# A four-layer graph network on one core: rows by block transposes and partition broadcasts, one statistics instruction per norm, and a plan with ranks

## The chip, the cores and the metric

The kernel runs on one core of one Trainium2 chip. The metric is the device time of one launch in microseconds. A core has a matrix engine (PE), a vector engine (DVE), a scalar engine (ACT), a general engine (POOL) and a queue that issues the DMAs here (SP); each works through its own instructions in program order and waits on semaphores for the others. PE's weight loads (PEld) stand beside its matmuls. PE writes to PSUM; the other tiles lie in SBUF.

## The reference

There are 64 independent graphs, each with 256 nodes and 256 features, all in fp32. A graph goes through four layers, and each layer ends in a residual sum and a layer norm. Cut to what matters:

```
for each of 64 graphs (x: 256x256, adj: 256x256):
  # layer 0: 4 heads, sigmoid attention scaled by row and column degrees
  q, k, v = lrelu(x Wq), lrelu(x Wk), lrelu(x Wlin + b)
  A_h = adj * sigmoid(q_h k_h^T / 8);  dis_h = rowsum(A_h)^-0.5
  x = norm(x + norm(dis_h * (A_h (dis_h * v_h))))
  # layer 1: 8 heads, masked softmax attention
  x = norm(x + (softmax(mask(q_h k_h^T / sqrt(32))) v_h) Wo + bo)
  # layer 2: neighbour sum, 256 -> 1024, rms norm, silu, 1024 -> 256
  h = (eps x + adj x) W1 + b1
  x = norm(x + silu(h * rsqrt(mean(h^2) + 1e-6) * w) W2 + b2)
  # layer 3: additive attention: e[i,j] = lrelu(s1[i] + s2[j])
  V = x W;  s1, s2 = V a1, V a2
  x = norm(x + gelu(norm(softmax(mask(e)) V) * gamma + beta))
```

Three of these quantities are needed as a row, that is, one value for each node along the free axis and the same on all partitions: the factor rsqrt(...) of layer 2 (hidden features lie on the partitions there), s2 of layer 3, and 1/sum of each head of layer 1 (its output lies with features on the partitions). Each comes into being as a column, with nodes on the partitions.

## The kernel before

**Graphs and operations.** The function `graph` describes one graph as a list of operations, each with an engine, a cost in ns that its author wrote beside it, the values that it reads and writes, and a closure that issues its instructions. `Plan.order` takes the operations of all 64 graphs together and makes one order of them: of those whose inputs are ready it takes the one with the lowest key, and it moves a clock for each engine by the written cost. The order so made is what the engines run. Several graphs are thus under way at once, each in another layer, and PE's work of one covers the other engines' work of the others. The key of an operation is this line, `start` being the earliest start by the plan's clocks and `due` a due time taken from the operations that follow it:

```
key = start, op.due, op.graph, op.index
```

**PE's modes.** Matmuls of layers 0 and 1 use part of the array: rows (L502, L582: queries times keys), or columns (L542, L618: attention times values; L520, L680: sums over partitions). The others use the full array (L368, L379, L649, L661, L707, L722). Transposes (`pe.transpose`, L323, L625, L693, L731) are matmuls against an identity. The plan has a price for each change of mode (`CHANGE`), and after rows or columns it starts operations of another mode later (`STAY`), to keep equal ones together.

**The rows.** In layer 2, `rs` (a column, two blocks of 128 nodes) is spread over 128 columns by a broadcast view and transposed by PE into the PSUM tile `pr` (L693, two instructions); DVE multiplies the hidden features by it (L697). In layer 3 the column s2 is spread in the same way (L731, two instructions, PSUM tile `ps2`), and ACT adds s1 to it and applies the leaky relu (L735). In layer 1, the reciprocals of 16 sums per node (8 heads, two blocks of nodes) are transposed by PE (L625), copied by ACT into `rT` (L627), written to DRAM by one DMA (L628) and read back by eight, one for each head, which spread a row of 256 over 32 partitions (L631, tile `rb`); DVE multiplies `av` by it (L635), which feeds the product with Wo (L379).

**The norms.** `stats` is called six times for each graph. For each of the two blocks of 128 nodes DVE runs `bn_stats` over 256 features (L393) and `bn_aggr` (L395); POOL adds 1e-5 (L405) and raises to the power -1/2 (L406). Where the sums of the softmax of layer 3 are folded in, DVE multiplies the variance twice by 1/sum (L401) and the result once (L409). Then `normed` or `affine` apply mean and factor, on ACT (L420, L445) or on DVE (L424, L453, L456).

**Transposes through DRAM.** Most large transposes aren't PE's: DVE transposes blocks of 32x32 (L335, L603), one DMA writes to a DRAM tile `far`, and four read it back.

**DMAs.** All come from SP's queue, in the plan's order.

Of the kernel before, what the change touches and what calls it, by code (L numbers as in the profile page):

```python
# [29 lines left out]
WORDS = {"s": 516, "d": 1024, "b": 2048, "c": 32, "p": 512, "h": 1024}  # L30
AHEAD = 12
STAY = 200
# [8 lines left out]
SLOTS = {"s": 42, "d": 10, "b": 3, "c": 72, "p": 8, "h": 8}  # L41
# [41 lines left out]
class Plan:  # L83
# [4 lines left out]
    def __init__(self, graphs):  # L88
        self.graphs = graphs
        self.ops, self.turns = [], {}  # L90
        self.graph = 0

    def op(self, engine, cost, fn, w=(), r=(), turn=None, mode="full", after=None, size=0, joint=None):

        pair = lambda x: (x[0], None if x[0].kind == "p" else x[1]) if isinstance(x, tuple) else (x, None)
        w, r = [pair(x) for x in w], [pair(x) for x in r]
        op = Op(engine, cost, fn, w, r, self.graph, turn, mode, after, size)
        op.table, op.joint, op.leaves = turn is not None and engine == "ACT", joint, mode
        if op.table:
            self.turns[turn] = self.turns.get(turn, 0) + 1  # L100
        self.ops.append(op)

# [42 lines left out]
    def order(self):  # L145
# [3 lines left out]
        for op in reversed(self.ops):  # L149
            op.due = min((nxt.due for nxt in op.after), default=4 * (min(op.graph + ROUND[3], self.graphs - 1 + TAIL[3]) + 1))  # L150
            if op.turn is not None:
                op.due = min(op.due, op.turn)
        clock = {e: 0.0 for e in AFTER}
# [6 lines left out]
        while ready:  # L160
            best = None
            for op in ready:
                if (op.due - AHEAD if op.first else op.turn or 0) > turns[turn]:
                    continue
                start = clock[op.engine]
                if op.engine == "PE" and mode in ("rows", "columns") and mode != op.mode:
                    start += STAY - 60 * (op.mode == "transpose")
                start = max(start, op.ready)
                need = {}
                for v in op.values:  # L170
                    if v.slot is None:
                        need[v.kind] = need.get(v.kind, 0) + 1
                for kind, n in need.items():
                    free = self.free[kind]
                    if len(free) < n:
                        break
                    start = max(start, sorted(free)[n - 1][0])
                else:
                    key = start, op.due, op.graph, op.index
                    if best is None or key < best[0]:  # L180
                        best = key, start, op
# [45 lines left out]
def weights(plan, nc, c, t):  # L227
# [32 lines left out]
    column("b1_q", "L1_gnn_bq"), column("b1_v", "L1_gnn_bv"), row("b1_o", "L1_gnn_bo")  # L260
# [37 lines left out]
def graph(plan, nc, c, t, out, b):  # L298
# [57 lines left out]

    def copy(ps, name):
        dst = Value("s", name, 2)
        op("ACT", 466, lambda: act.copy(dst.t, ps.t), [dst], [ps])  # L359
        return dst  # L360
# [26 lines left out]
    def stats(src, r=None):  # L387


        mv, st = Value("c", "mv", 2), Value("c", "st", 2)  # L390
        m = lambda: mv.t[:, :6].rearrange("p (n k) -> p n k", n=2)
        for n in range(NB):
            op("DVE", 328, lambda n=n: dve.bn_stats(st.t[:, 6 * n:6 * n + 6], two(src)[:, n, :]), [(st, n)], [(src, n)])  # L393
        for n in range(NB):
            op("DVE", 82, lambda n=n: dve.bn_aggr(m()[:, n, 0:2], st.t[:, 6 * n:6 * n + 6]), [(mv, n)], [(st, n)])  # L395

        r2 = lambda: r.t[:, :NB]
        if r:
            def fn():
                for _ in range(2):  # L400
                    dve.tensor_tensor(m()[:, :, 1], m()[:, :, 1], r2(), OP.mult)  # L401
            op("DVE", 250, fn, [mv], [mv, r])

        def fn():
            pool.tensor_scalar(m()[:, :, 2], m()[:, :, 1], 1e-5, None, op0=OP.add)  # L405
            pool.tensor_tensor(m()[:, :, 2], m()[:, :, 2], c.mhalf[:, :NB], OP.pow)  # L406
        op("POOL", 1010, fn, [mv], [mv], after=580)
        if r:
            op("DVE", 60, lambda: dve.tensor_tensor(m()[:, :, 2], m()[:, :, 2], r2(), OP.mult), [mv], [mv, r])  # L409
        return mv, m  # L410

    def normed(src, name):
        mv, m = stats(src)
        dst = Value("s", name, 2)
        if name != 'o' or b >= plan.graphs - ENDS:
            op("DVE", 70, lambda: dve.scalar_tensor_tensor(  # L416
                m()[:, :, 0], m()[:, :, 0], -1.0, m()[:, :, 2], op0=OP.mult, op1=OP.mult), [mv], [mv])
        for n in range(NB):
            if name != 'o' or b >= plan.graphs - ENDS:
                op("ACT", 492, lambda n=n: act.activation(  # L420
                    two(dst)[:, n, :], two(src)[:, n, :], AF.Identity, bias=m()[:, n, 0:1], scale=m()[:, n, 2:3]),
                    [(dst, n)], [(src, n), mv])
                continue
            op("DVE", 328, lambda n=n: dve.tensor_scalar(  # L424
                two(dst)[:, n, :], two(src)[:, n, :], m()[:, n, 0:1], m()[:, n, 2:3],
                op0=OP.subtract, op1=OP.mult), [(dst, n)], [(src, n), mv])
        return dst
# [11 lines left out]
    def affine(y, mv, m, g, add, r=(), src=None):  # L439

        if src and b >= plan.graphs - ENDS:
            op("DVE", 70, lambda: dve.scalar_tensor_tensor(
                m()[:, :, 0], m()[:, :, 0], -1.0, m()[:, :, 2], op0=OP.mult, op1=OP.mult), [mv], [mv])
            for n in range(NB):
                op("ACT", 491, lambda n=n: act.activation(  # L445
                    two(y)[:, n, :], two(src)[:, n, :], AF.Identity, bias=m()[:, n, 0:1], scale=m()[:, n, 2:3]),
# [5 lines left out]
        for n in range(NB):  # L452
            op("DVE", 395, lambda n=n: dve.scalar_tensor_tensor(  # L453
                two(y)[:, n, :], two(src)[:, n, :], m()[:, n, 0:1], g.t, op0=OP.subtract, op1=OP.mult),
                [(y, n)], [(src, n), mv, g])
            op("DVE", 395, lambda n=n: dve.scalar_tensor_tensor(  # L456
                two(y)[:, n, :], two(y)[:, n, :], m()[:, n, 2:3], add(n), op0=OP.mult, op1=OP.add),
# [107 lines left out]
    ps = feature_major(c.w1_q, xT)  # L565
    qT1 = Value("s", "qT1", 2)
    for o in range(2):
        op("ACT", 357, lambda ps=ps, o=o: act.activation(
            two(qT1)[:, o, :], two(ps)[:, o, :], AF.Identity, bias=c.b1_q.t[:, o:o + 1]), [(qT1, o)], [(ps, o), c.b1_q])

    kT1 = copy(feature_major(c.w1_k, xT), "kT1")
# [3 lines left out]
    for hq in range(H1 // 4):  # L575
# [9 lines left out]
        for pair in range(2):  # L585
            e = Value("d", "e", 4)
            for i in range(2):
                softmax(pss[2 * pair + i], negmask, HD1 ** -0.5, e,
                        lambda n, i=i, e=e: e.t[:, 256 * (2 * i + n):256 * (2 * i + n + 1)],
                        lambda n, i=i: 2 * i + n, r, lambda n, h=4 * hq + 2 * pair + i: 2 * h + n, turn(1, EXP))  # L590
# [22 lines left out]
    def fn():  # L613
# [10 lines left out]
    ps = Value("p", "ps")  # L624
    op("PE", PE_TR, lambda ps=ps: pe.transpose(ps.t[:16, :P], r.t[:, :16], c.ident), [ps], [r], mode="transpose")  # L625
    rT, far, rb = Value("s", "rT"), Value("h", "far"), Value("s", "rb", H1)
    op("ACT", 160, lambda ps=ps: act.copy(rT.t[:16, :P], ps.t[:16, :P]), [rT], [ps])  # L627
    op("SP", 470, lambda far=far: nc.sync.dma_start(far.t[:2].rearrange("q (g m) -> (q g) m", m=P), rT.t[:16, :P]),  # L628
       [far], [rT], after=2000, size=8)
    for h in range(H1):  # L630
        op("SP", 470, lambda h=h, far=far: nc.sync.dma_start(  # L631
            two(rb)[h % 4 * HD1:(h % 4 + 1) * HD1, h // 4, :],
            far.t[h // 4:h // 4 + 1, h % 4 * N:(h % 4 + 1) * N].to_broadcast([HD1, N])), [(rb, h)], [far], after=1700, size=32)
    yT = Value("s", "yT")
    op("DVE", 575, lambda: dve.tensor_tensor(yT.t, av.t, rb.t, OP.mult), [yT], [av, rb])  # L635
# [3 lines left out]
    for n in range(NB):  # L639
        d = lambda n=n: two(adj2)[:, n, n * P:(n + 1) * P]  # L640
        op("DVE", 200, lambda d=d: dve.tensor_tensor(d(), d(), c.eps_id.t, OP.add), [(adj2, n)], [(adj2, n), c.eps_id])
# [47 lines left out]
    pr = Value("p", "pr")  # L689

    def fn():
        for n in range(NB):
            pe.transpose(pr.t[:, n * P:(n + 1) * P], rs.t[:, n:n + 1].to_broadcast([P, P]), c.ident)  # L693
    op("PE", 2 * PE_TR, fn, [pr], [rs], mode="transpose")
    for j in range(0, HB, 4):
        four = [(hT, i) for i in range(j, j + 4)]
        op("DVE", 1130, lambda j=j: dve.tensor_tensor(  # L697
            Hb(j, 4), Hb(j, 4), pr.t[:, None, :N].to_broadcast([P, 4, N]), OP.mult), four, [*four, pr])
# [28 lines left out]
    ps2 = Value("p", "ps2")  # L727

    def fn():
        for n in range(NB):  # L730
            pe.transpose(ps2.t[:, n * P:(n + 1) * P], V3()[:, n, D + 1:D + 2].to_broadcast([P, P]), c.ident)  # L731
    op("PE", 2 * PE_TR, fn, [ps2], [v3], turn=turn(3, EXP), mode="transpose")
    e = Value("s", "e3", 2)
    for n in range(NB):
        op("ACT", 360, lambda n=n: act.activation(two(e)[:, n, :], ps2.t[:, :N], AF.Prelu, bias=s1(n), alpha=0.2),  # L735
           [(e, n)], [ps2, v3])
# [16 lines left out]
def gnn_stack_kernel(ctx: ExitStack, tc: tile.TileContext, t: dict, out: bass.AP):  # L753
# [20 lines left out]
        {"space": {"p": bass.MemoryType.PSUM, "h": bass.MemoryType.DRAM}[kind]} if kind in "ph" else {})))  # L774
# [4 lines left out]
    make_identity(nc, ident)  # L779
# [57 lines left out]
```

## Time and profile before

| what | value |
|---|---|
| median of 3 runs (2696.18 to 2699.69) | 2696.62 us |
| the profiled execution, first to last instruction | 2698.6 us |
| PE busy, share of the span | 2666.0 us, 99% |
| DVE busy | 2436.7 us, 90% |
| ACT busy | 2228.8 us, 83% |
| POOL busy | 588.5 us, 22% |
| DMA queue of SP, share of 16 engines | 67.0% |
| mean granted TensorE clock | 0.997 |

The page gives no time of its own for the profiled execution beyond its span, which is 2.0 us above the median of the runs. "Busy" counts the time in which at least one instruction of the engine is under way. Matmuls overlap, so a busy PE is read further down by the distance between the starts of its instructions.

### The profile page before, as it was taken

Reading aid. Unit: us, or ns where it says so; the run is one execution under the profiler, and the core shown is the slowest. Engines: PE = TensorE matmul, PEld = TensorE weight load, DVE = VectorE, ACT = ScalarE, POOL = GpSimd, SP = SyncE. Lnnn points to the kernel's source line nnn. Section 1 sums busy time; section 2 is a strip of 40 time slices with the busy share of each in tenths; the row PEclk is TensorE's granted clock in tenths of the full one; section 3 lists DMA queues with packets and bytes.
Section 4 is the critical chain, followed back from the end, with each engine's and each line's share of the span. In section 5 each row is a group of like instructions: output and inputs, shape, how many; then the busy total and the mean of one; then the engine's idle time right before and its main releaser. Section 6 shows DMA issues by size and latency. Waiting matters only on the chain.

```text
span 2698.6 us, 56499 instructions
## 1 busy us (share of the span) xinstructions
PE 2666.0 (99%) x17568; PEld 2144.9 (79%) x17568; DVE 2436.7 (90%) x7480; ACT 2228.8 (83%) x5343; POOL 588.5 (22%) x902
## 2 busy tenths in 40 slices
PE   8999999999999999999999999999999999999997
PEld 6777788887887878878888878888788788787776
DVE  6789999999899999999999999989999899999986
ACT  4888888888888988888888888888888888888886
POOL 1111222212222212222222222222222222222212
PEclk9999999999999999999999999999999999999999
DMA  4476875766767767667767677677676676776661
GB/s 146 133 213 176 219 219 161 211 192 183 200 185 187 215 178 189 196 181 207 202 169 206 186 190 212 173 190 201 172 213 193 169 212 189 186 212 181 169 173 36
DMA packets 708045, 501.01 MB, mean 186 GB/s; under 512 B 309792, under 2 KB 667552, under 8 KB 707744
## 3 DMA queue, kind: packets, MB, share of 16 engines
q1 hardware_dynamic: 707744, 497.40, 67.0%
q8 instruction: 140, 2.29, 0.4%
q14 instruction: 161, 1.32, 0.2%
HBM read 301.35 MB, written 195.82 MB: 184 GB/s over the span
## 4 chain that ended last, share of the span: by engine, by line
PE 93%; DVE 3%; ACT 2%; DMA 1%; SPq 1%; issue 1%; POOL 0%; ACTq 0%; POOLq 0%; DVEq 0%
PE ps L368 16%; PE ps L707 16%; PE ps L661 16%; PE ps L379 15%; PE ps L582 5%; PE ps L502 4%; PE ps L542 4%; PE av L618 4%; PE ps L722 4%; PE ps L649 4%; PE ps L323 1%; PE ps L520 1%; PE pr L693 1%; DVE e L465 1%; PE ps L731 0%
## 5 line engine op out<-in xcount | busy, mean ns | idle before, releaser
L470 ACT ACTIVATE e<-e,low 128x256 f32<-128x256 f32 x1152 | 574.6, 500 | 83.7 <-DVE low L465 82.9
L707 PE MATMUL ps<-w,hT 128*128 128x256 f32 x2048 | 466.8, 380 | 1.3 <-ACT hT L699 1.2
L661 PE MATMUL ps<-aggT,w 128*128 128x256 f32 x2048 | 463.4, 380 | 1.6 <-ACT aggT L359 1.0
L707 PEld LDWEIGHTS ps<-w,hT 128*128 128x128 f32 x2048 | 385.7, 190 | 60.4 <-issue 4.6
L661 PEld LDWEIGHTS ps<-aggT,w 128*128 128x128 f32 x2048 | 383.3, 190 | 57.0 <-issue 2.8
L405 POOL TENSOR_SCALAR mv<-mv 128x2 f32<-128x2 f32 x384 | 127.8, 333 | 1316.8 <-DVE mv L395 888.0
L465 DVE CUSTOM_DVE_ANT_0 e<-ps,adj 128x256 f32<-128x256 f32 x1024 | 361.7, 418 | 30.0 <-PE ps L582 29.9
L406 POOL TENSOR_TENSOR mv<-mv,mhalf 128x2 f32<-128x2 f32 x384 | 306.0, 797 | 32.0
L603 DVE STREAM_TRANSPOSE eb<-e 128x1024 f32<-128x1024 f32 x248 | 300.8, 1221 | 0.8 <-ACT e L470 0.7
L668 ACT ACTIVATE hT<-ps,br,r 128x256 f32<-128x256 f32 x512 | 255.7, 585 | 33.9 <-PE ps L707 30.6
L393 DVE BATCH_NORM_STATS2 st<-y 128x6 f32<-128x256 f32 x640 | 238.3, 408 | 1.2
L420 ACT ACTIVATE x<-y,mv 128x256 f32<-128x256 f32 x384 | 215.2, 600 | 28.9 <-DVE mv L416 26.1
L666 ACT ACTIVATE sq<-ps,b 128x256 f32<-128x256 f32 x512 | 220.0, 474 | 20.2 <-PE ps L661 19.7
L470 ACT ACTIVATION_READ_ACCUMULATOR e<-e,low 128x1 f32 x1152 | 219.0, 190 | 0.0
L508 DVE TENSOR_TENSOR att<-att,adjT 128x512 f32<-128x512 f32 x256 | 166.4, 676 | 10.0 <-ACT att L506 10.0
L688 POOL TENSOR_TENSOR rs<-rs,mhalf 128x2 f32<-128x2 f32 x64 | 45.6, 712 | 540.4 <-DVE rs L686 518.9
L528 POOL TENSOR_TENSOR dp<-dp,mhalf 128x8 f32<-128x8 f32 x64 | 110.2, 1722 | 215.8 <-DVE dp L527 168.3
L697 DVE TENSOR_TENSOR hT<-hT,pr 128x1024 f32<-128x1024 f32 x128 | 150.0, 1210 | 5.2 <-PE pr L693 4.3
L582 PE MATMUL ps<-kT,qT 32*128 32x256 f32 x2048 | 146.2, 399 | 0.0
L673 DVE TENSOR_TENSOR sq<-sq 128x512 f32<-128x512 f32 x192 | 129.5, 675 | 11.1 <-ACT sq L666 10.2
L368 PE MATMUL ps<-x0T,w_q 128*128 128x256 f32 x512 | 130.4, 385 | 6.6 <-DMA x0T<-in_xT 6.6
L506 ACT ACTIVATE att<-ps 128x512 f32<-128x512 f32 x256 | 132.2, 603 | 3.8 <-PE ps L502 3.1
(119 smaller groups left out, 5508.9 us busy)
## 6 DMA issues: line engine op xcount, KB each, us to landing
far<-eb SPq DMA_DIRECT2D x248, 512.0 KB, 3.6
eT<-far SPq DMA_DIRECT2D x992, 128.0 KB, 4.1
adj<-in_adj SPq DMA_DIRECT2D x128, 256.0 KB, 5.1
far<-eb SPq DMA_DIRECT2D x488, 64.0 KB, 2.0
x0T<-in_xT SPq DMA_DIRECT2D x64, 256.0 KB, 4.7
adjT<-in_adjT SPq DMA_DIRECT2D x64, 256.0 KB, 4.9
x<-in_x SPq DMA_DIRECT2D x64, 256.0 KB, 5.2
adj<-in_adjT SPq DMA_DIRECT2D x64, 256.0 KB, 4.8
```

Of the source, the lines that this page charges most:

```text
L368: pe.matmul(two(ps)[:, o, :], w.t[:, k, o * P:(o + 1) * P], two(xT)[:, k, :], start=(k == 0), stop=(k == DB - 1))
L379: pe.matmul(two(ps)[:, n, :], two(xT)[:, k, n * P:(n + 1) * P], w()[:, k, :], start=(k == 0), stop=(k == DB - 1))
L393: op("DVE", 328, lambda n=n: dve.bn_stats(st.t[:, 6 * n:6 * n + 6], two(src)[:, n, :]), [(st, n)], [(src, n)])
L406: pool.tensor_tensor(m()[:, :, 2], m()[:, :, 2], c.mhalf[:, :NB], OP.pow)
L465: op("DVE", 345, lambda n=n: dve.tensor_tensor_reduce(out=E(n), in0=two(logits)[:, n, :], in1=two(negmask)[:, n, :], scale=-scale, scalar= ...
L470: op("ACT", 491, lambda n=n: act.activation(E(n), E(n), AF.Exp, bias=low.t[:, n:n + 1], scale=-1.0, accum_out=r.t[:, col(n):col(n) + 1]), ...
L582: pe.matmul(two(pss[i])[:, n, :], two(qT1)[s, hq, n * P:(n + 1) * P], two(kT1)[s, hq, :], start=True, stop=True)
L603: op("DVE", 1155, lambda e=e, eb=eb: dve.transpose(eb.t.rearrange("p (b g i) -> p g b i", b=4, i=32), e.t.rearrange("p (g b i) -> p g b i" ...
L661: pe.matmul(two(ps)[:, i, :], c.w2_1.t[:, k, (j + i) * P:(j + i + 1) * P], two(aggT)[:, k, :], start=(k == 0), stop=(k == DB - 1))
L666: op("ACT", 357, lambda ps=ps, sq=sq, i=i, j=j: act.activation(two(sq)[:, i, :], two(ps)[:, i, :], AF.Square, bias=c.b2_1.t[:, j + i:j + i ...
L668: op("ACT", 491, lambda ps=ps, i=i, j=j: act.activation(Hb(j + i)[:, 0], two(ps)[:, i, :], AF.Identity, bias=c.br2.t[:, j + i:j + i + 1], ...
L707: pe.matmul(two(ps)[:, n, :], Hb(j)[:, 0, n * P:(n + 1) * P], c.w2_2.t[:, j, :], start=(j == 0), stop=(j == HB - 1))
```

## The change

The rows of layers 2 and 3 are made by a new function, `row_of`: DVE transposes blocks of 32x32 of a broadcast view of the column, after which the first partition of each group of 32 holds 32 values of each block; four POOL instructions (`partition_broadcast`) then copy one group's partition to all 128. The row is a tile in SBUF instead of PSUM. POOL loads a library of instructions for it at the start of the kernel. The identity is made by a POOL `iota` and a DVE comparison, in place of a POOL memset and a POOL selection.

The reciprocals of layer 1 are transposed by DVE in blocks of 32x32 and written to DRAM by one DMA with 128 runs of 64 values; the eight DMAs that spread them read runs of 64 values instead of runs of 256. `yT` is made by two DVE instructions, one for each block of nodes.

`stats` runs one `bn_stats` over both blocks, with the two blocks' features interleaved by the view; its even and odd halves are the two blocks. `bn_aggr` goes. What follows reads the sum of squared deviations (third word of three) and multiplies by 1/256 and adds 1e-5 in one DVE instruction, so POOL keeps only the power. 

Of the smaller edits: the keys of layer 1 get their bias (b1_k), by two ACT instructions instead of one copy; eps is added to the diagonal blocks of the adjacency by one DVE instruction instead of two.

In the plan, each operation gets a rank: its kind is the line of its closure, its engine and which of its kind in the graph it is, 335 kinds in all. Two lists have a number for each kind; LEAD is added to the start and RANK to the due time in the key. AHEAD, STAY and the discount for transposes after rows or columns have other values.

```diff
-from concourse.masks import make_identity
+from concourse import library_config, mybir
...
-WORDS = {"s": 516, "d": 1024, "b": 2048, "c": 32, "p": 512, "h": 1024}
-AHEAD = 12
-STAY = 200
+WORDS = {"s": 516, "d": 1024, "b": 2048, "c": 32, "p": 512, "h": 1024, "t": 64, "w": 256, "f": 64}
+AHEAD = 12.7
+STAY, TURN_STAY = 197, 988
...
-SLOTS = {"s": 42, "d": 10, "b": 3, "c": 72, "p": 8, "h": 8}
+SLOTS = {"s": 42, "d": 10, "b": 3, "c": 72, "p": 8, "h": 8, "t": 5, "w": 3, "f": 8}
+DRAM = "hf"
+
+RANK = [
+    3.44, -1.34, 0, 0.79, 3.63, 0, 7.06, 0, 0, 2.3, -1.09, 0.34, 2.1, 0.78, 0.47, 0, -8.07, 0, -2.5, 0, 15.95,
...
+LEAD = [
+    0, 0, 0, 4, 0, 21, 963, 0, 0, 0, 63, 0, 36, -156, 0, 241, -51, 5, -54, -409, 0, 480, 0, -31, 0, 0, -1244, 5,
...
+        kind = fn.__code__.co_firstlineno, engine
+        n = self.seen.get((self.graph, kind), 0)
+        self.seen[self.graph, kind] = n + 1
+        op.kind = kind, n
...
-                    start += STAY - 60 * (op.mode == "transpose")
+                    start += STAY - TURN_STAY * (op.mode == "transpose")
...
-                    key = start, op.due, op.graph, op.index
+                    key = start + LEAD[op.rank], op.due + RANK[op.rank], op.graph, op.index
...
+    def row_of(column, src, name):
+
+        blocks, row = Value("t", "blocks"), Value("w", name, 4)
+        op("DVE", 110, lambda: dve.transpose(
+            blocks.t.rearrange("p (n k) -> p n k", n=NB), column().to_broadcast([P, NB, 32])), [blocks], src)
+        for a in range(4):
+            op("POOL", 300, lambda a=a: pool.partition_broadcast(
+                row.t.rearrange("p (n a k) -> p n a k", n=NB, a=4)[:, :, a],
+                blocks.t[32 * a:32 * a + 1].rearrange("p (n k) -> p n k", n=NB)), [(row, a)], [blocks], after=250)
+        return row
...
-        mv, st = Value("c", "mv", 2), Value("c", "st", 2)
+        mv = Value("c", "mv")
...
-        for n in range(NB):
-            op("DVE", 328, lambda n=n: dve.bn_stats(st.t[:, 6 * n:6 * n + 6], two(src)[:, n, :]), [(st, n)], [(src, n)])
-        for n in range(NB):
-            op("DVE", 82, lambda n=n: dve.bn_aggr(m()[:, n, 0:2], st.t[:, 6 * n:6 * n + 6]), [(mv, n)], [(st, n)])
+        op("DVE", 615, lambda: dve.bn_stats(mv.t[:, :6], src.t[:, :512].rearrange("p (n c) -> p c n", n=NB)), [mv], [src])
...
-            pool.tensor_scalar(m()[:, :, 2], m()[:, :, 1], 1e-5, None, op0=OP.add)
-            pool.tensor_tensor(m()[:, :, 2], m()[:, :, 2], c.mhalf[:, :NB], OP.pow)
-        op("POOL", 1010, fn, [mv], [mv], after=580)
+            dve.tensor_scalar(m()[:, :, 0], m()[:, :, 2], 1.0 / D, 1e-5, op0=OP.mult, op1=OP.add)
+        op("DVE", 300 if r else 60, fn, [mv], [mv] + [r] * bool(r))
+        op("POOL", 720, lambda: pool.tensor_tensor(m()[:, :, 0], m()[:, :, 0], c.mhalf[:, :NB], OP.pow), [mv], [mv], after=400)
...
-    qT1 = Value("s", "qT1", 2)
-    for o in range(2):
-        op("ACT", 357, lambda ps=ps, o=o: act.activation(
-            two(qT1)[:, o, :], two(ps)[:, o, :], AF.Identity, bias=c.b1_q.t[:, o:o + 1]), [(qT1, o)], [(ps, o), c.b1_q])
-
-    kT1 = copy(feature_major(c.w1_k, xT), "kT1")
+    for w, bias, name in ((c.w1_q, c.b1_q, "qT1"), (c.w1_k, c.b1_k, "kT1")):
+        ps, y = feature_major(w, xT), Value("s", name, 2)
+        for o in range(2):
+            op("ACT", 357, lambda ps=ps, y=y, bias=bias, o=o: act.activation(
+                two(y)[:, o, :], two(ps)[:, o, :], AF.Identity, bias=bias.t[:, o:o + 1]), [(y, o)], [(ps, o), bias])
...
-    op("PE", PE_TR, lambda ps=ps: pe.transpose(ps.t[:16, :P], r.t[:, :16], c.ident), [ps], [r], mode="transpose")
-    rT, far, rb = Value("s", "rT"), Value("h", "far"), Value("s", "rb", H1)
-    op("ACT", 160, lambda ps=ps: act.copy(rT.t[:16, :P], ps.t[:16, :P]), [rT], [ps])
-    op("SP", 470, lambda far=far: nc.sync.dma_start(far.t[:2].rearrange("q (g m) -> (q g) m", m=P), rT.t[:16, :P]),
-       [far], [rT], after=2000, size=8)
+    rT, far, rb = Value("t", "rT"), Value("f", "far"), Value("s", "rb", H1)
+    op("DVE", 110, lambda: dve.transpose(
+        rT.t.rearrange("p (n k h) -> p n k h", n=NB, h=H1),
+        r.t[:, :16].rearrange("p (n h) -> p n h", n=NB)[:, :, None, :].to_broadcast([P, NB, 4, H1])), [rT], [r])
+    op("SP", 470, lambda far=far: nc.sync.dma_start(far.t, rT.t), [far], [rT], after=2000, size=32)
     for h in range(H1):
         op("SP", 470, lambda h=h, far=far: nc.sync.dma_start(
-            two(rb)[h % 4 * HD1:(h % 4 + 1) * HD1, h // 4, :],
-            far.t[h // 4:h // 4 + 1, h % 4 * N:(h % 4 + 1) * N].to_broadcast([HD1, N])), [(rb, h)], [far], after=1700, size=32)
-    yT = Value("s", "yT")
-    op("DVE", 575, lambda: dve.tensor_tensor(yT.t, av.t, rb.t, OP.mult), [yT], [av, rb])
+            two(rb)[h % 4 * HD1:(h % 4 + 1) * HD1, h // 4, :].rearrange("p (a m) -> p a m", a=4),
+            far.t.rearrange("(a c) m -> c a m", a=4)[h][None].to_broadcast([HD1, 4, 64])),
+            [(rb, h)], [far], after=2000, size=40)
+    yT = Value("s", "yT", 2)
+    for n in range(NB):
+        op("DVE", 350, lambda n=n: dve.tensor_tensor(
...
-    for n in range(NB):
-        d = lambda n=n: two(adj2)[:, n, n * P:(n + 1) * P]
-        op("DVE", 200, lambda d=d: dve.tensor_tensor(d(), d(), c.eps_id.t, OP.add), [(adj2, n)], [(adj2, n), c.eps_id])
+    d = lambda: adj2.t.rearrange("p (g w) -> p g w", g=4)[:, ::3]
+    op("DVE", 322, lambda: dve.tensor_tensor(d(), d(), c.eps_id.t[:, None, :].to_broadcast([P, NB, P]), OP.add),
+       [adj2], [adj2, c.eps_id])
...
-    pr = Value("p", "pr")
-
-    def fn():
-        for n in range(NB):
-            pe.transpose(pr.t[:, n * P:(n + 1) * P], rs.t[:, n:n + 1].to_broadcast([P, P]), c.ident)
-    op("PE", 2 * PE_TR, fn, [pr], [rs], mode="transpose")
+    pr = row_of(lambda: rs.t[:, :NB, None], [rs], "pr")
...
-    ps2 = Value("p", "ps2")
-
-    def fn():
-        for n in range(NB):
-            pe.transpose(ps2.t[:, n * P:(n + 1) * P], V3()[:, n, D + 1:D + 2].to_broadcast([P, P]), c.ident)
-    op("PE", 2 * PE_TR, fn, [ps2], [v3], turn=turn(3, EXP), mode="transpose")
+    s2 = row_of(lambda: V3()[:, :, D + 1:D + 2], [v3], "s2")
...
-    make_identity(nc, ident)
+    apart = const.tile([P, P], mybir.dt.int32, name="apart")
+    nc.gpsimd.load_library(library_config.all_libraries[10])
+    nc.gpsimd.iota(apart, [[-1, P]], base=0, channel_multiplier=1)
+    nc.vector.tensor_scalar(ident, apart, 0, None, op0=OP.is_equal)
```

## The prediction

> **What bounds the kernel now.** I read the page's busy times first, then the chain that ended last.
>
> ```profile
> PE 2666.0 (99%) x17568; PEld 2144.9 (79%) x17568; DVE 2436.7 (90%) x7480; ACT 2228.8 (83%) x5343; POOL 588.5 (22%) x902
> ...
> PE 93%; DVE 3%; ACT 2%; DMA 1%; SPq 1%; issue 1%; POOL 0%; ACTq 0%; POOLq 0%; DVEq 0%
> ```
>
> PE is on 93% of the chain. Whether it is full or only looks busy, the distances between its starts tell. A piece of the chain in mid-run, in order of time (start, length, what):
>
> ```profile
> 1380.08 6.91 PE ps L707 x32
> 1386.98 1.93 PE ps L502 x16
> 1388.91 0.21 PE ps L625
> 1389.12 3.46 PE ps L379 x16
> 1392.58 0.22 PE ps L731 x2
> 1392.80 0.57 PE ps L520 x16
> 1393.37 0.59 PE ps L323 x4
> 1393.96 6.05 PE ps L368 x28
> ```
>
> Nothing but PE stands there. 6.91 us / 32 is 216 ns a matmul instruction, and 3.46/16 and 6.05/28 are the same: no gaps. So I took each start-to-start distance of the trace apart by what follows what. Medians: full array to full array 216 ns, full to rows or columns 309, rows to full or to a transpose 305, transpose to transpose or to full 109. Added up over the old order these give 2636.4 us; from PE's first start (6.57 us) to its last (2682.8) the trace has 2676.2. **PE's waits are 39.8 us in all**: 12.9 in the first 200 us, 8.9 from 2500 on, 18 in the 2300 between (0.3 for each graph). Before the first start lie 6.6 us, after the last 15.8 (the last graph's norms and the output). 6.6 + 2636.4 + 39.8 + 15.8 = 2698.6, the span.
>
> The next engine, by stretch of the run (PE, PEld, DVE, ACT, POOL busy):
>
> ```profile
> 400.00:1400.00 1000.00, 999.64 (x6616) 807.13 (x6618) 926.39 (x2832) 840.46 (x2012) 222.45 (x337) 1.00 0.70 192
> ```
>
> DVE has 7.4% free, 3.0 us of a graph's 41.2 us (2636/64). That is the reserve to watch.
>
> **What the Trainium skill says.** "TensorEngine Tiling (Array Packing)", Key Properties: changing the tiling mode drains TensorE. The trace agrees: 309 against 216 ns on the way in, 305 on the way out. "VectorE: DVE Perf Modes", The three transpose paths: DVE transposes only within 32x32 blocks; hence the four broadcasts for each row. "SBUF — State Buffer", Who interferes with whom: a DVE instruction with two SBUF inputs and a GpSimd instruction that reads SBUF block each other for a whole instruction. The trace fits: L405's median is 221 ns, its mean 333, its longest 1427. "GPSIMD Engine Reference", Instruction dispatch: the first call of a freshly loaded kernel costs about 6 us that the profile doesn't show; no run here shows it.
>
> **The change, part by part.**
>
> *Transposes off PE.* These go:
>
> ```profile
> L693 PE MATMUL pr<-ident,rs 128*128 128x128 f32 x128 | 26.1, 285 | 0.2 <-POOL rs L688 0.2
> L731 PE MATMUL ps<-ident,v 128*128 128x128 f32 x128 | 24.6, 274 | 0.0
> L625 PE MATMUL ps<-ident,r 128*16 128x128 f32 x64 | 17.7, 277 | 0.0
> ```
>
> The busy sum, 68.4 us, is not what PE gets back, since matmuls overlap. For each of these blocks I took the distance from the start before it to the start after it, less what those two would be apart without it: L693 16.1 us, L731 14.3, L625 9.6, in sum **40.0 us**, all on the bounding engine.
>
> *The new order.* The built program's order of instructions shows what the lists did on PE. Starts of one kind after another, before and after, times the distances above: rows to full 79 to 137, columns to full 46 to 81, rows to columns 14 to 52, full to rows 120 to 136; against that rows to transpose 95 to 3, columns to transpose 34 to 5, full to columns 117 to 87, full to transpose 134 to 73, transpose to full 246 to 78, transpose to transpose 405 to 267. In all the new order costs 2596.7 us, 39.7 less than the old one. Removing the transposes in place gives 40.0, so the lists change next to nothing on PE's own work: **what they bring must come out of the 39.8 us of waits.**
>
> *Norms on DVE.*
>
> ```profile
> L393 DVE BATCH_NORM_STATS2 st<-y 128x6 f32<-128x256 f32 x640 | 238.3, 408 | 1.2
> L395 DVE BATCH_NORM_AGGREGATE mv<-st 128x2 f32<-128x6 f32 x768 | 115.7, 165 | 0.0
> L405 POOL TENSOR_SCALAR mv<-mv 128x2 f32<-128x2 f32 x384 | 127.8, 333 | 1316.8 <-DVE mv L395 888.0 <-DVE mv L401 236.1 <-DVE rs L686 29.0
> ```
>
> With the 128 that read PSUM (48.6 us), 402.6 us go. 384 instructions of 512 elements come; a 128x512 tensor_tensor takes 675 ns (L673), twice the old instruction would be 816; I take 675: 259.2. The added multiply-add is 128x2 as L686, 154 ns: 59.1. Net -84.3 us (-30 at 816). POOL loses 127.8 us.
>
> *Other DVE work.* 128 block transposes of 128x64 for the rows and 64 for layer 1, at 245 ns (L685): +47.1. `yT`: 64 of 677 ns become 128 of 408 (L553): +8.9. The diagonal: -4.9. **DVE in sum: -33 us** (+21 at 816 ns), 0.5 us a graph. It stays behind PE.
>
> *ACT.* kT1 37.5 us becomes 54.7 as L568 has, the copy L627 (15.8) goes: +1.4 us, hidden by ACT's 16% free.
>
> *POOL.* 512 broadcasts of 64 values. The trace has none. From below the smallest POOL instruction, 0.21 us (L405); from above the power over 8 values, 1.72 us (L528). I take 0.4: +205 us, POOL at 25%; at 1.72, 50%. As throughput harmless; as latency it counts in a chain. In the new order PE has 16.3 us (median) from the sums of squares (L680's successor) to the first product that needs the row. The chain between: 0.5 to DVE, 0.25 transpose, 0.15, POOL's power 0.7, 0.25 transpose, four broadcasts, 1.2 multiply (L697), 1.3 table load and 1.05 silu on ACT, some 0.8 of handovers: 6.2 us and the four. At 0.4 that is 7.8 of 16.3; even at 1.72 it is 13. Row s2 has 35.4 us. `yT` is tightest: its product starts 3.19 us after the attention product's start both before and after; before, 0.36 to 0.47 us stood between the end of `yT` and the product where 0.15 is the least seen, so 0.2 to 0.3 were free. Two halves take 0.13 more (2 x 0.41 against 0.69). It fits.
>
> *DMA.* `rb` reads 1024 runs of 256 B a graph instead of 256 of 1 KB, the write has 128 runs instead of 16: +880 packets a graph, 56,320 in all, at 41 ns each (67% of 16 engines' span over 707,744 packets) 5 points: 67 to 72%. The count of issues on SP is nearly the same. Hidden, since the old `rb` landed in 1.9 us and the softmax-to-product link has 62 us; if landings grew by 3 us, the order still has them.
>
> *The start.* DVE's identity comparison stands fourth in its queue and waits for POOL's iota, which waits for the library; adjacency, residual and attention work stand behind it. DVE's first such work began at 13.4 us. Below 0 for a library ready by then; with 25 us, some 10 us of PE waits. I take 0.
>
> *The end.* Each of the last norms saves one POOL instruction (0.22) and 0.4 on DVE, some -1 us of the 15.8; the last row costs about as much more than the PE transpose did.
>
> *Sum.* 2698.6 - 39.7 = 2658.9 with the old waits. Of these, 21.8 lie at the two ends; that the lists take away 8 is an estimate (bounds: 20 less, 20 more). Span 2651, and 2.0 less as the median stood to the profiled span: **2649 us**.
>
> **Rivals.**
>
> *A new small wait in every period.* The new order repeats strictly: for most links the median slack equals the 90th percentile. A wait that recurs costs 64 times: 0.3 us (`yT` behind a busy DVE, a late `rb`) are 19 us, 0.5 are 32: 2668 to 2690. For it: `yT`'s thin margin. Against it: the old order, nearly as regular, shows 0.3 a graph from all causes.
>
> *Slower: DVE stands behind the broadcasts.* The order places DVE's multiply L697 after broadcasts of 300 ns. If they take longer, DVE waits with its queue behind it, and its free 3.0 us a graph (3.5 after) are used up. Where all of the excess is waited for, two rows of four make 8(b - 0.3); layer 3's row is read by ACT, so half of it falls on DVE directly, half through e3. It is past the reserve at b = 0.74 us. At b = 1.0, 5.6 - 3.5 = 2.1 us a graph, 134 us: 2783. Shared-port blocking works the same way, since `pr` as a second SBUF input now makes L697 contend. Against it: 16.3 us of slack leave the order room to have had other DVE work first.
>
> *The change moves PE's time into waits.* 0.62 us a graph lost anywhere gives 2697, no change.
>
> **How the numbers follow.** PE-bound with waits of 20 to 50 us, 2630 to 2668: 0.62. Small recurring wait or a late start, up to 2690: 0.24. Within 0.2% of before (2691.2 to 2702.0; about what a measurement of this kernel can tell from no change): 0.04. Slower: 0.10. Range 2630 to 2690, 2649 likeliest.
>
> **What would show it.** PE's rows L625, L693 and L731 gone, PE busy near 2600 and still at 98 to 99%; distances of 216 and 305 to 309 ns unchanged; bn_stats near 0.68 us; DVE near 2400. A broadcast beyond 0.7 us with DVE idle "<-POOL pr" would make the slower rival right; PE waiting each period on `yT`, the first. PE's busy share under 97% would mean that another engine has taken over.

## The result, and the profile after

The changed kernel takes 2666.8 us in the median (2666.0 to 2668.8) against 2697.2 us before, measured again beside it: ratio 0.988, 95% interval 0.987 to 0.990. A second comparison of the same two kernels gave 0.987 (0.986 to 0.989). The gain is 30 us, the forecast was 48 us (2649 us, with a range of 2630 to 2690).

The page of the changed kernel, busy times and the chain that ended last:

```profile
PE 2629.6 (99%) x17248; PEld 2122.6 (80%) x17248; DVE 2463.8 (92%) x6905; ACT 2246.5 (84%) x5343; POOL 640.5 (24%) x1029
...
PE 89%; DVE 5%; DMA 2%; SPq 1%; issue 1%; ACT 1%; POOL 1%; POOLq 0%; DVEq 0%; ACTq 0%
```

PE lost 320 instructions (17,568 to 17,248, the 320 transposes) and 36 us of busy time and is still full. DVE did not get lighter, as the prediction had it, but 27 us heavier. The middle of the run, by stretch (PE, PEld, DVE, ACT, POOL busy):

```profile
400.00:1400.00 1000.00, 1000.00 (x6584) 812.82 (x6583) 952.20 (x2662) 857.00 (x2049) 244.05 (x393) 1.00 0.73 195
```

PE has no gap there at all, and DVE has 4.8% free instead of 7.4%. The new instructions, in the groups by line:

```profile
L445 DVE BATCH_NORM_STATS2 mv<-y 128x6 f32<-128x512 f32 x320 | 217.3, 692 | 0.6
L453 DVE TENSOR_SCALAR mv<-mv 128x2 f32<-128x2 f32 x384 | 58.9, 165 | 4.2
L745 DVE TENSOR_TENSOR hT<-hT,pr 128x1024 f32<-128x1024 f32 x128 | 149.1, 1202 | 2.2 <-POOL pr L405 2.1
L405 POOL PARTITION_BROADCAST s<-blocks x256 | 89.7, 435 | 185.8 <-DVE mv L452 147.5 <-DVE blocks L402 27.7 <-DVE r L672 4.5
L405 POOL PARTITION_BROADCAST pr<-blocks x256 | 65.5, 370 | 183.9 <-DVE blocks L402 183.4
L778 ACT ACTIVATE e<-s,v 128x256 f32<-128x256 f32 x128 | 57.6, 495 | 10.7 <-POOL s L405 10.7
```

A norm's statistics take 692 ns, a broadcast 370 to 435. The four of a layer-2 row take 1.0 us together, since they overlap; in 49 of the 64 layer-3 rows a power of a norm stands between them, and they take 2.5 us. In the whole run DVE waits 2.1 us for its row and ACT 10.7 us for the row s2.

**The term that the sum lacked.** A piece of the chain in mid-run:

```profile
1387.26 1.93 PE ps L702 x8
...
1390.05 1.08 PE ps L631 x16
1391.12 1.92 PE ps L432 x8
1393.05 1.73 PE ps L714 x8
```

Eight full-array instructions take 1.73 us behind full-array work and 1.92 behind rows (L631). Of the 0.19 us more, the prediction had 89 ns, the first distance (305 against 216). The other 104 lie one step further: **the second full-array instruction starts 320 ns after the first instead of 216.** In the two traces this holds for 124 of 125 and for 218 of 218 changes from rows or columns to the full array (behind columns the first distance is 203 ns in the median, and the second again 320). Behind a transpose that itself follows rows or columns it does not appear: the distances are then 305, 114 and 218 ns instead of 305 and 320, so that the transpose of 16 columns adds 12 ns in all. There the prediction's own fence shows `L625` and then 16 instructions in 3.46 us. On the way into rows the same step stands: in both kernels the second pair of instructions of L502 (now L550) starts 313 ns after the first, later pairs 209, and the second four of L582 (now L631) 300 ns after the first, later ones 196.

With this term (and 5 to 50 ns for transposes in that place) the account of both profiled executions follows. All distances are medians of the trace of before, taken by what stands ahead and behind; a negative wait means that the starts came a little sooner than these medians.

| us | before | after |
|---|---|---|
| before PE's first start | 6.6 | 6.1 |
| PE's starts by the order | 2653.0 | 2619.8 |
| waits of PE: first 300 us, to 2200, rest | 11.4, 2.5, 9.3 | 11.3, -1.0, 12.7 |
| after PE's last start | 15.8 | 15.2 |
| span | 2698.6 | 2664.2 |

PE's work fell by 33.2 us and its waits did not change. The 23.2 us of waits before are 16.6 less than the 39.8 that the prediction read: those 16.6 us were distances of PE's own that its sum lacked. The profiled execution of before lay some 3 us higher than its kernel's median (the changed kernel's own profiled run took 2666.0 us with a span of 2664.2), so the spans differ by 34 us and the medians by 30.

### The profile page after: what moved, and what is told of

Its sections match the earlier page's. It is cut to its first block, busy times and chain, and to the rows that moved or that the text cites. A ratio compares the mean times of both kernels' runs of the same rounds, so it can differ in the third digit from the quotient of the medians.

```text
span 2664.2 us, 54927 instructions
## 1 busy us (share of the span) xinstructions
PE 2629.6 (99%) x17248; PEld 2122.6 (80%) x17248; DVE 2463.8 (92%) x6905; ACT 2246.5 (84%) x5343; POOL 640.5 (24%) x1029
## 3 DMA queue, kind: packets, MB, share of 16 engines
q1 hardware_dynamic: 764336, 498.97, 69.7%
## 4 chain that ended last, share of the span: by engine, by line
PE 89%; DVE 5%; DMA 2%; SPq 1%; issue 1%; ACT 1%; POOL 1%; POOLq 0%; DVEq 0%; ACTq 0%
PE ps L432 16%; PE ps L755 15%; PE ps L421 15%; PE ps L714 15%; PE ps L631 5%; PE ps L702 4%; PE ps L550 4%; PE ps L590 4%; PE av L667 4%; PE ps L770 4%; PE ps L365 1%; PE ps L568 1%; DVE mv L445 1%; DVE e L513 1%; DMA eT<-far 1%
## 5 line engine op out<-in xcount | busy, mean ns | idle before, releaser
L455 POOL TENSOR_TENSOR mv<-mv,mhalf 128x2 f32<-128x2 f32 x384 | 313.7, 822 | 965.7 <-DVE mv L453 759.8
L755 PE MATMUL ps<-w,hT 128*128 128x256 f32 x2048 | 456.4, 380 | 0.0
L445 DVE BATCH_NORM_STATS2 mv<-y 128x6 f32<-128x512 f32 x320 | 217.3, 692 | 0.6
L576 POOL TENSOR_TENSOR dp<-dp,mhalf 128x8 f32<-128x8 f32 x64 | 126.6, 1978 | 161.6 <-DVE dp L575 161.3
L631 PE MATMUL ps<-kT,qT 32*128 32x256 f32 x2048 | 147.8, 400 | 0.0
L554 ACT ACTIVATE att<-ps 128x512 f32<-128x512 f32 x256 | 138.8, 600 | 3.9 <-PE ps L550 3.2
L421 PE MATMUL ps<-x0T,w_k 128*128 128x256 f32 x512 | 131.9, 385 | 6.1 <-DMA w_k<-in_L_gnn_W_k 6.1
L747 ACT ACTIVATE hT<-hT 128x1024 f32<-128x1024 f32 x128 | 133.3, 1051 | 3.4 <-DVE hT L745 2.7
```

The lines of the kernel that those rows point to most:

```text
L421: pe.matmul(two(ps)[:, o, :], w.t[:, k, o * P:(o + 1) * P], two(xT)[:, k, :], start=(k == 0), stop=(k == DB - 1))
L445: op("DVE", 615, lambda: dve.bn_stats(mv.t[:, :6], src.t[:, :512].rearrange("p (n c) -> p c n", n=NB)), [mv], [src])
L455: op("POOL", 720, lambda: pool.tensor_tensor(m()[:, :, 0], m()[:, :, 0], c.mhalf[:, :NB], OP.pow), [mv], [mv], after=400)
L631: pe.matmul(two(pss[i])[:, n, :], two(qT1)[s, hq, n * P:(n + 1) * P], two(kT1)[s, hq, :], start=True, stop=True)
L755: pe.matmul(two(ps)[:, n, :], Hb(j)[:, 0, n * P:(n + 1) * P], c.w2_2.t[:, j, :], start=(j == 0), stop=(j == HB - 1))
```

## The experiments

The theory to be tried, R: PE is the bound, a change is worth what it takes off PE's starts, and a transpose behind a tiled block (one of rows or columns) costs almost nothing, since it bears the restart, that is, it stands in place of the longer second distance. Rivals: T, every transpose costs its 109 ns; D, an in-order DVE with little room makes PE wait; L, the lists work on waits. "Order" below is the emission order; where it says that it is kept, the plan is the same and only what an operation issues was edited.

### What a transpose costs, by its place

A run of the changed kernel as the mark, and two with idle transposes added in the same order:

> The changed kernel itself, as the mark for the others of this call. Both theories: 2667 us, 0.988 of before, PE's starts stretching over some 2643 us.

```diff
+            if dst and mode in ("rows", "columns"):   # e1; e2: mode == "full", 2 of 15
+                nc.tensor.transpose(dst(), ident, ident)
             op.fn()
```

> The changed kernel in the same order; ahead of 215 full-array blocks that directly follow rows or columns, PE makes one more 128x128 transpose of the identity into the tile that the block is about to overwrite. Theory R (restart): the first full matmul behind a tiled block costs 104 ns more before the second can start, and a transpose in that place bears it instead; 215 transposes cost 109 + 5 - 104 = 10 ns each, 2 us in all: 2669 us. Theory T (a transpose costs its 109 ns wherever it stands, as the sum of the prediction had it): 23 us, 2690 us. Theory D (DVE is the bound, PE has room): nothing, 2667 us.

> The changed kernel in the same order; 217 such transposes, but ahead of full-array blocks that follow a full-array block, evenly spread over the run. Theories R and T: 109 ns each, 23.7 us: 2690 us. Theory D: nothing or a few us, below 2672 us.

And, after their results, the same as the first with 16 columns:

```diff
-                nc.tensor.transpose(dst(), ident, ident)
+                nc.tensor.transpose(dst()[:16, :], ident[:, :16], ident)
```

> The changed kernel in the same order, 215 more transposes just behind rows or columns as before, but of 16 columns into 16 partitions, as L625 had. With 128 columns each cost 44 ns there and 96 ns inside the full array. Theory R: the small weight load is done in 88 ns instead of 136, so a transpose costs 109 + 5 - 104 = 10 ns: 2 us in all, 2668 us. Theory T: 23 us, 2690 us. If it costs 44 ns as the large one, 2675 us, the width of the load does not matter.

| kernel | median us | more than the mark, for each transpose |
|---|---|---|
| the changed kernel again | 2666.1 | |
| 217 inside full-array work, 128 columns | 2686.9 | 96 ns |
| 215 behind rows or columns, 128 columns | 2675.5 | 44 ns |
| 215 behind rows or columns, 16 columns | 2665.9 | -1 ns |

The same instruction costs 96, 44 or about no ns by its place and the width of its weights. T and D fall for this question. The last kernel was run apart from the mark; taken against the kernel before in each set it comes to 6 ns, and runs of one kernel lie 2 to 3 us to either side of the median, 9 to 14 ns for each transpose, so R's 10 ns are not excluded. The traces tell it closer: three starts lie 305, 165 and 218 ns apart with 128 columns, 305, 114 and 218 with 16, where 305 and 320 stand without a transpose. That is 63 and 12 ns more; inside full-array work it is 111. The chain of the last kernel shows it beside the fence above (L862 is the added transpose, L704 is L702 there):

```profile
1388.87 0.21 PE ps L862
1389.08 1.73 PE ps L704 x8
```

0.21 + 1.73 is 1.94, where the block alone took 1.93. With 128 columns 44 ns were paid instead of the 10 that R expected; the full-array start then follows the transpose by 165 ns instead of 114, and the wider weight load takes 138 ns instead of 87, the same 51 ns more.

### One part alone: the reciprocals of layer 1

```diff
-    op("PE", PE_TR, lambda ps=ps: pe.transpose(ps.t[:16, :P], r.t[:, :16], c.ident), [ps], [r], mode="transpose")
+    op("PE", PE_TR, lambda: None, [ps], [r], mode="transpose")
...
-    op("ACT", 160, lambda ps=ps: act.copy(rT.t[:16, :P], ps.t[:16, :P]), [rT], [ps])
+    op("ACT", 160, lambda: dve.transpose(rT.t[:, :64]..., r.t[:, :16]...), [rT], [ps])
...
```

> The kernel before, in its own order, with one part of the change alone: the reciprocals of layer 1 are transposed by DVE (issued where ACT's copy stood), written as 128 runs of 64 values, read back in runs of 64, and yT is made by two DVE instructions. 64 transposes leave PE. Theory R: 60 of the 64 stood just behind rows or columns, so their going uncovers the restart of the full array; PE's starts come to 2651.8 us against 2653.0, 1.2 us less, time 0.9995 of before. Theory T: 7 us (64 x 109 ns) to the 9.6 us of the prediction, 0.9965 to 0.9974. Rival Q: late rb tiles add waits, slower than before.

Measured 2699.6 us, ratio 1.001 (1.000 to 1.0015); PE's starts by the order 2651.8, waits 23.7. Taking 64 transposes off PE won nothing measurable, and T falls. R's 1.2 us less show in the starts and not in the time: its 0.9995 lies just under the interval. Q's late tiles don't show either, with 23.7 us of waits against 23.2. The place where L625 stood in the prediction's fence, now:

```profile
1386.33 1.93 PE ps L502 x16
1388.26 3.65 PE ps L379 x16
```

3.65 instead of 0.21 + 3.46.

### One part alone: the statistics

> The kernel before, in its own order, with the new statistics alone (one bn_stats, the multiply-add on DVE, the power on POOL); rows as before. PE's work is the old one, 2653.0 us of starts. Theory P and D2: PE's waits in mid-run are near nothing already, so nothing to win: 0.998 to 1.001 of before. Rival S (the statistics are worth their 33 us in any order): 0.988.

```diff
-            op("DVE", 82, lambda n=n: dve.bn_aggr(...), [(mv, n)], [(st, n)])
+            op("DVE", 82, second, [(mv, n)], [(st, n)])   # issues the one bn_stats, at the second call
...
-            pool.tensor_scalar(m()[:, :, 2], m()[:, :, 1], 1e-5, None, op0=OP.add)
+            dve.tensor_scalar(m()[:, :, 0], m()[:, :, 2], 1.0 / D, 1e-5, op0=OP.mult, op1=OP.add)
```

2701.3 us, ratio 1.001 (1.000 to 1.002): nothing won where PE's work stays.

### The statistics of before in the changed order

```diff
-        op("DVE", 615, lambda: dve.bn_stats(mv.t[:, :6], src.t[:, :512].rearrange(...)), [mv], [src])
+        def old():   # two bn_stats, two bn_aggr, into the same tile
+            ...
+        op("DVE", 615, old, [mv], [src])
```

> The changed kernel in the same order, with the statistics of before on DVE: two bn_stats and two bn_aggr for each norm instead of one bn_stats; POOL as in the changed kernel. By start-to-start distances DVE gets 252 + 70 - 242 = 80 us more at most, 1.25 us a graph, of 1.95 that it has free in mid-run. Theory P (PE is the bound and DVE's room covers it): 0 to 10 us slower, 2667 to 2677 us. Rival D (the room is not usable, since DVE's order is fixed and its idle time is waiting for PE and ACT): most of the 80 us, 2700 us and above.

2699.4 us, 33 us slower than the changed kernel: the whole gain is gone. PE's order is the same to the instruction, its waits grow from 23 to 55 us. The largest single part of the 32 us more, groups by line, the changed kernel and then this one:

```profile
L432 PE MATMUL ps<-w_o,yT 128*128 128x256 f32 x512 | 122.6, 381 | 0.9 <-DVE yT L685 0.9
```

```profile
L432 PE MATMUL ps<-w_o,yT 128*128 128x256 f32 x512 | 126.2, 388 | 10.8 <-DVE yT L690 10.8
```

That is the link which the prediction called tightest, now with 50 waits of some 0.2 us each. The other 22 us are spread over many lines. P with its 10 us falls, D with most of the 80 us too: about two fifths were paid, though DVE was still under 98% busy in mid-run:

```profile
400.00:1400.00 1000.00, 995.19 (x6548) 801.63 (x6540) 971.21 (x3062) 850.03 (x2015) 232.89 (x387) 1.00 0.73 193
```

### Later rows: every broadcast twice

> The changed kernel in the same order; every partition_broadcast is issued twice. POOL has 155 us more, 30% busy, and each row comes 1.5 to 1.8 us later. Theory P: the rows have slack, 0 to 5 us slower, 2667 to 2672 us. Rival B (DVE and ACT stand behind the broadcasts, or the shared port stops DVE): two rows of 1.6 us a graph, up to 200 us; any of it over 10 us speaks for it.

```diff
+                for _ in range(2):
                     pool.partition_broadcast(...)
```

2737.7 us, 71 us slower, with PE's order the same and its waits at 92 us. DVE's group in this kernel:

```profile
L748 DVE TENSOR_TENSOR hT<-hT,pr 128x1024 f32<-128x1024 f32 x128 | 151.5, 1222 | 81.5 <-POOL pr L407 79.6 <-ACT v L415 1.8
```

DVE stands 79.6 us behind the row where it stood 2.1. The rival B is right: each of 128 rows takes 1.8 us longer (in layer 2 its broadcasts take 2.8 us together instead of 1.0), 230 us in all, and 71 us of it are paid. Of B's two ways it is the wait: DVE's busy time did not grow (2462.3 us against 2463.8), so broadcasts that hold up DVE's own instructions don't show.

### The order

> The changed kernel with its operations, but the plan's key without RANK and LEAD and with AHEAD, STAY and the discount for transposes as before. Theory R: the order that comes out has 273 exits from rows or columns to the full array instead of 218 and more changes of mode; at the measured distances, with 104 ns more for each exit, PE's starts come to 2636.1 us instead of 2619.8, so 16 us slower at equal waits: 2683 us. Rival L (the lists work by taking waits away at the ends): PE's own work about as with the lists, and 8 to 20 us more of waits in the first and last 200 us. Rival N (the lists matter little): 2667 to 2672 us.

```diff
-AHEAD = 12.7
-STAY, TURN_STAY = 197, 988
+AHEAD = 12
+STAY, TURN_STAY = 200, 60
...
-                    key = start + LEAD[op.rank], op.due + RANK[op.rank], op.graph, op.index
+                    key = start, op.due, op.graph, op.index
```

2745.3 us, 79 us slower than with the lists and 1.6% slower than before. PE's starts by the order are 2636.1 us, the 16.3 more that R had; but its waits are 86.7 us, 64 more. R was right on PE's work and wrong on "equal waits". L's 8 to 20 us at the two ends came out (some 15), but between 300 and 2200 us stand 47.5 us where there were none, which no theory had, and PE's own work was not "about as with the lists". The lists (319 numbers each, not 335) and the three constants went back together; what each of them does was not tried. The largest group of waits, changed kernel and this one:

```profile
L432 PE MATMUL ps<-v,eT 128*128 128x256 f32 x512 | 127.1, 391 | 2.6 <-ACT eT L412 1.9 <-DMA eT<-far 0.7
```

```profile
L432 PE MATMUL ps<-v,eT 128*128 128x256 f32 x512 | 131.1, 400 | 21.0 <-DMA eT<-far 11.2 <-ACT eT L412 3.7 <-DVE sq L726 3.6
```

### All rows off PE, in the order of before

> The kernel before, in its own order, with all three rows off PE: as in the run on the reciprocals, and besides the rows of layers 2 and 3 by a DVE block transpose and four POOL broadcasts, issued where PE's transposes stood. Statistics and lists as before. Theory R: PE's starts come to 2625.8 us, 27 us less than before: 2670 us at equal waits. Theory T: 40 us less, 2657 us. Rival Q: the broadcasts stand in an order that was not made for them, waits grow by 10 us and more, 2680 us or above.

The edits are those for the reciprocals, and at the place of PE's transposes for the other rows:

```diff
-            pe.transpose(pr.t[:, n * P:(n + 1) * P], rs.t[:, n:n + 1].to_broadcast([P, P]), c.ident)
+        pr.row = row_of(rs.t[:, :NB, None], "pr")
...
```

3797.4 us. None of the theories had it. POOL's timeline in this kernel:

```profile
1399.81 0.69 POOL L706 TENSOR_TENSOR rs<-rs,mhalf 128x2 f32<-128x2 f32 x1 [9.23 <-DVE rs L704]
1406.59 1.02 POOL L361 PARTITION_BROADCAST row<-blocks  x4 [6.09 <-issue]
1415.03 0.24 POOL L414 TENSOR_SCALAR mv<-mv 128x2 f32<-128x2 f32 x1 [7.42 <-issue]
1415.36 0.74 POOL L415 TENSOR_TENSOR mv<-mv,mhalf 128x2 f32<-128x2 f32 x1
```

POOL stands 6 to 7 us without a visible reason at each change to and from the broadcasts. The built program has a load of a library at these places, and the trace has two records of POOL's sequencer (MODIFY_POOL_CONFIG) for each. There are 250 of them: 125 ahead of broadcasts, 85 ahead of TENSOR_SCALAR and 40 ahead of the power (TENSOR_TENSOR with mhalf). The changed kernel has one, ahead of the iota, and its power and broadcasts then alternate without another. This fits a library with the broadcasts that lacks TENSOR_SCALAR. If so, moving the 1e-5 from POOL to DVE, which the prediction had only counted as 128 us of POOL time, is what lets the broadcasts stay loaded. Two more runs without that loss; they take over the iota as well, so the two edits were tried together only:

```diff
-            pool.tensor_scalar(m()[:, :, 2], m()[:, :, 1], 1e-5, None, op0=OP.add)
+            dve.tensor_scalar(m()[:, :, 2], m()[:, :, 1], 1e-5, None, op0=OP.add)
...
-    make_identity(nc, ident)
+    nc.gpsimd.iota(apart, [[-1, P]], base=0, channel_multiplier=1)   # and is_equal on DVE
```

> The kernel before, in its own order, all three rows off PE as in the run that took 3797 us, with two things of the change more: DVE adds the 1e-5 of the norms instead of POOL, and the identity comes from the iota. POOL then runs nothing that its loaded library lacks; the program has one load ahead of the iota instead of one at every change between broadcasts and other work. Theory C (the 6 to 8 us at every such change were the loss): the 1.1 ms go; with theory R for PE, starts come to 2625.8 us, 2670 us at equal waits, up to 2690 us if DVE's 20 us more and the later rows cost waits as the doubled broadcasts did. Rival Q (the broadcasts stand in an order not made for them, and that was the loss): still above 2750 us. Theory T: 2657 us.

> As the run beside it, with the new statistics instead of bn_stats twice and bn_aggr twice: all parts of the change in the order of before, without any planning for them. DVE has some 44 us less by start-to-start distances. Theory P (PE alone is the bound): the same time as the run beside it, within 4 us. Theory D2 (an in-order DVE with under 8% free makes PE wait, as the old statistics did with 33 us in the changed order): 10 to 25 us faster than the run beside it.

2812.2 and 2775.4 us. C is right: 985 us go, and one load is left. The rest isn't R's 2670: PE's starts by the order are 2625.8 us, 27 less than before, but its waits are 162 and 124 us. ACT's group in the first of the two, the leaky relu that reads row s2:

```profile
L751 ACT ACTIVATE e<-row,v 128x256 f32<-128x256 f32 x128 | 58.0, 500 | 132.5 <-POOL row L361 130.8 <-DMA eT<-far 1.7
```

Q is right here: in an order made for a row that PE delivers at once, ACT stands behind POOL, 130.8 us against the 10.7 of the changed kernel. DVE also has 80 us more to do than before (2516.4 against 2436.7 us busy); the new statistics take 61 of them away and are worth 37 us in this order, more than the 10 to 25 of D2, and nothing in the order of before with its old rows. So with all three parts and no planning (the smaller edits left out) the kernel is 2.8% slower than before (2775 us); planned with the new costs but without lists and with the old constants, 1.6% slower (2745); with both, 1.2% faster (2667).

## Why the prediction was right or wrong

**The bound.** Right: PE stayed full, and the gain is what left its starts. 2666.8 us lies at the upper edge of the case that was called likeliest (2630 to 2668), with 30 us gained of the 48 forecast.

**40.0 us for the transposes in place, 39.7 for the new order.** Mis-sized, for lack of the 104 ns. The changes from rows or columns straight to the full array rise from 125 to 218. With the term the order saves 33.2 us, 6.5 less. The in-place values fall to 1.2 us (L625, by the run on the reciprocals), 12.8 (L693) and 13.9 (L731); by the order of the runs with all rows off PE the three are 27.2 us together. PE's busy time came to 2629.6 us; the "near 2600" does not follow from the prediction's own 40 us, which would make it 2626.

**The waits.** Misread: of the 39.8 us, 16.6 were PE's own distances. In mid-run, where it had 0.3 us for each graph, there was next to nothing to take away (2.5 us from 300 to 2200 us). The estimate of 8 us less failed: 23.2 before, 23.0 after. Together with 4.6 us for how medians stand to spans (2.0 below expected, 2.6 above found) and 1.1 less at start and end, these make the 17.8 us between 2649 and 2666.8: 6.5 + 7.8 + 4.6 - 1.1.

**"The lists change next to nothing on PE's own work."** Wrong. With the full account the transposes alone take 27.2 us off the starts in the old order and the new order takes 33.2, so 6.0 us are the order's. Against the order that the plan makes of the same operations without lists and with the old constants, it is 16.3 us of PE's work and 64 us of waits.

**DVE -33 us.** Wrong in sign: +27, beyond its own bound of +21. The group of bn_aggr counted 115.7 us, but from start to next start it held DVE for 70.1, since it overlaps with what follows; bn_stats 252.1. The new pair takes 242.3 and 35.7, so the norms gave back 44 us, not 84. The block transposes for the rows cost 32 (47 expected), `yT` 8, and the diagonal gave back 6. Some 36 us came back in instructions that the change left alone, 24 of them in small ones that overlap less with the next: the reciprocal L672 holds DVE 242 ns instead of 159, L739 146 instead of 67.

**"It stays behind PE."** Right in the changed kernel, but its free time was no reserve: 80 us more of DVE work cost 33 us. That a sum 60 us too low did no harm to the forecast is luck. The changed plan has 615 ns written for the one bn_stats, and 615 is also the median from its start to the next in the trace, so there the order was made for the duration that the trace shows, which the prediction did not use.

**Rows with 16.3 us on PE against a chain of 8.** Failed as an argument. The distance on PE is no slack when DVE's multiply is placed just behind the row; of 1.8 us more for each row nearly a third was paid. The mechanism of the slower rival is thus real, and only its size kept it out: the four broadcasts of a layer-2 row take 1.0 us.

**The rest.** `yT`'s margin held (0.9 us of waits), but not with the statistics of before (10.8 us), so the first rival's small recurring wait is real too. DMA went from 67.0 to 69.7%, 72 expected, with `rb` landing in 3.2 us instead of 1.9 and the write ahead of it in 4.4 instead of 2.0. POOL is at 24%, 25 expected. At the start nothing was lost: the iota ran at 0.9 us. Two figures of the prediction don't fit its own sum: "no change" takes 0.75 us a graph from 2649 (0.62 holds with the old waits), and 2630 stands for waits of 13 us, not 20. The 6 us that "GPSIMD Engine Reference", Instruction dispatch, states for a first call agree in size with the gaps at POOL's loads in the kernel with 250 of them (medians of 6.1 us ahead of broadcasts and 7.2 ahead of TENSOR_SCALAR); the changed kernel, with its one load, has 0.43 us ahead of the iota.

## What to carry to other kernels

Price an instruction by what the starts around it become without it, and look two instructions past a change of mode; one that bears a restart is nearly free, and removing it wins next to nothing. In engines that run in a fixed order, neither the idle time of an engine that is 95% busy nor a long distance on the bound engine is slack: in this kernel 80 us of DVE work and 1.8 us for each row cost 33 and 71 us. Nor does freed time become a gain by itself: the same statistics won nothing where PE hardly waited, 37 us where it waited, and 33 in the order made for them. Before an instruction is moved to POOL, see in the trace whether a load stands between it and its neighbours.

## What the runs showed of the hardware that was not expected

- Behind rows or columns the second full-array instruction starts 320 ns after the first (216 elsewhere), in 342 of 343 cases; with a transpose of 16 columns first, the whole way from rows to the full array is 12 ns longer, no more. On the way into rows the second group of instructions also starts 104 ns late (313 against 209, 300 against 196). What in PE causes it was not tried.
- A change between POOL libraries cost 5.7 to 7.8 us between one instruction's end and the next one's start in 212 of 250 cases in one run; the others, up to 20 us, may hold other waits.
- Short DVE instructions overlap with the next: bn_aggr, 165 ns in the trace, holds DVE for 91 ns from start to next start in the kernel before.
- An idle 128-column transpose costs 96 ns inside full-array work and 44 behind rows or columns.
